# First stage of a graph network with two columns of nodes per transposition and per matmul

## The chip, the cores and the metric

The kernel runs on one NeuronCore of a Trainium2 chip. Times are device microseconds (us). Three runs of the kernel before took 4300.02, 4304.88 and 4320.17 us; the median is 4304.88 us. The engines are named PE (TensorE, matmuls), ACT (ScalarE), DVE (VectorE), POOL (GpSimd) and SP (SyncE, which here only issues DMAs). Each engine works through its own instructions in the order in which they were laid down; engines wait for one another through semaphores.

## What is computed

One layer of a message-passing graph network with attention, on 12,500 nodes of 64 features and 412,500 edges sorted by receiver:

```
h  = relu(layernorm(x))
m  = concat(h[src], h[dst], edge)                 # 64 + 64 + 32 features
messages = silu(m @ W1 + b1) @ W2 + b2            # 64
logit    = silu(m @ Wa1 + ba1) @ Wa2 + ba2        # 1
att      = softmax(logit over all edges)
agg      = segment_sum(messages * att, dst)
out = x + silu(concat(h, agg) @ Wu1 + bu1) @ Wu2 + bu2
```

The products of m with W1 and Wa1 split into a part of the sender, a part of the receiver and a part of the edge. So the kernel makes two tables of 128 values per node first: ts = h @ [Wa1, W1] of the sender's rows, and tr of the receiver's rows, and then adds, for each edge, one row of ts, one of tr and the edge's own product.

## The kernel before

**Stage one, the tables.** The nodes are padded to 12,544 and laid out as 128 partitions of NB = 98 columns: column b of all partitions is a set of 128 nodes. They are worked in 7 chunks of CB = 14 columns. The loop at L200 normalises a chunk: DVE sums it (L205) and subtracts the mean (L208), ACT squares (L210), DVE sums again (L212), ACT takes the root (L214), DVE inverts (L215) and multiplies with the relu in one pass, giving h (L217). Then, in blocks of four columns, PE transposes each column of h (L224), DVE copies the four transposed columns from PSUM to the tile hT (L225), PE multiplies each with the sender's weights (L228), and ACT copies the result from PSUM to the tile ts (L230). hT has 65 rows: 64 features and a row of ones (L184, a memset on POOL), through which the matmul adds the biases, which are the last row of w_node (L98 to L109). At the end of a chunk SP stores ts to the table ts_d in DRAM (L231), and ACT's queue stores hT to hT_d (L232), to be read again much later by `node_bias`.

A second loop (L233) multiplies the same hT, column by column, with the receiver's weights (L240), DVE copies the results (L242), and ACT's queue stores them to tr_d (L243). `keep_in_program_order` holds these matmuls behind those of the first loop.

`windows()` (L186 to L198) computes from the receivers' numbers where each edge's receiver lies in its window: eight DVE instructions, the largest over 128 x 3224 values (L188). It is called ahead of the third chunk.

**Stage two, the edges.** `one_pass` takes 403 groups of K = 8 x 128 edges. For each group POOL issues eight indirect DMAs (L358), each of which gathers 128 rows of ts_d by the senders' numbers into the tile gs, of which there are 8 buffers. Edges are sorted by receiver, so a group's receivers lie in a window of tr_d that SP loads (L377); DVE builds a one-hot matrix (L379) and one matmul per 256 edges (L385) gives the receiver's and the edge's parts together. DVE adds them to gs (L390), ACT takes the tanh (L391), DVE forms the messages and logits (L399 to L407), and some groups later a weighted sum into the nodes follows (L442 to L481). Every fourth group from the 16th on also runs `node_bias` (h @ Wu1 + bu1 for four columns of nodes, from hT_d) or `node_rest`. A last stage updates the nodes (L572 on).

**What sets the order.** The program is written as above, but a planner lays down each engine's list by its own estimate of when things are ready, within the dependences, except where `keep_in_program_order` (`pin`) fixes it. So DVE, ACT and SP have the instructions of neighbouring chunks mixed, and where a call stands in the text is not where its instructions stand in the list. DMAs of SP and of ACT go to two queues, which share the 16 DMA engines, and each DMA instruction takes one of eight semaphores in turn, so that an issue can also wait for an earlier DMA of the same semaphore. The gathers wait for the whole of ts_d, since any edge can ask for any row.

Of the kernel before, what the change touches and what calls it, by code (L numbers as in the profile page):

```python
# [40 lines left out]
F32 = mybir.dt.float32  # L42
I32 = mybir.dt.int32
AF = mybir.ActivationFunctionType
ALU = mybir.AluOpType
# [5 lines left out]
P = 128  # L51
D = 64
DE = 32
U = 64
C = 2 * U
# [19 lines left out]
def gnn_kernel(ctx: ExitStack, tc: tile.TileContext, n_edges, x, src, dst, dst_row, first, edge,  # L75
# [14 lines left out]
    hT_d = dram.tile([D, NB, P], F32, name="hT_d")  # L90
# [7 lines left out]
    w_node = const.tile([D + 1, 2 * C + U], F32, name="w_node")  # L98
    nc.vector.memset(w_node[D:D + 1, C:2 * C], 0.0)
    nc.sync.dma_start(w_node[:D, 0:U], Wa1[0:D, :])  # L100
    nc.sync.dma_start(w_node[:D, U:C], W1[0:D, :])
    nc.sync.dma_start(w_node[D:D + 1, 0:U], ba1[None, :])
    nc.sync.dma_start(w_node[D:D + 1, U:C], b1[None, :])
    nc.scalar.dma_start(w_node[:D, C:C + U], Wa1[D:2 * D, :])
    nc.scalar.dma_start(w_node[:D, C + U:2 * C], W1[D:2 * D, :])
    nc.scalar.dma_start(w_node[:D, 2 * C:], Wu1[0:D, :])
    nc.scalar.dma_start(w_node[D:D + 1, 2 * C:], bu1[None, :])

    nc.vector.tensor_scalar(w_node[:, 0:2 * C], w_node[:, 0:2 * C], 0.5, None, op0=ALU.mult)  # L109
# [12 lines left out]
    def across(ap, n, name, dtype=F32, parts=P):  # L122
        t = const.tile([parts, n], dtype, name=name)
        nc.scalar.dma_start(t, bass.AP(tensor=ap.tensor, offset=ap.offset, ap=[[0, parts], [1, n]]))
        return t

    wa2 = across(Wa2, U, "wa2")
# [40 lines left out]
    with tc.tile_pool(name="node1", bufs=1) as node1, \  # L168
# [14 lines left out]
        hT = node1.tile([D + 1, NB, P], F32, name="hT")  # L183
        nc.gpsimd.memset(hT[D:D + 1], 1.0)  # L184
# [14 lines left out]

        for c in range(0, NB, CB):  # L200
            if c == min(2 * CB, NB - CB):
                windows()
# [17 lines left out]
            for b in range(0, CB, 4):  # L220
                n = min(4, CB - b)
                pt = node_ps.tile([D, 4, P], F32, name="pt")
                for i in range(n):
                    nc.tensor.transpose(pt[:, i, :], h[:, b + i, :], ident)  # L224
                nc.vector.tensor_copy(hT[:D, c + b:c + b + n, :], pt[:, :n, :])  # L225
                pn = node_ps.tile([P, 4, C], F32, name="pn")
                for i in range(n):
                    nc.tensor.matmul(pn[:, i, :], hT[:, c + b + i, :], w_node[:, 0:C],  # L228
                                     start=True, stop=True)
                nc.scalar.copy(ts[:, b:b + n, :], pn[:, :n, :])  # L230
            nc.sync.dma_start(ts_d.rearrange("(p b) f -> p b f", b=NB)[:, c:c + CB, :], ts)  # L231
            nc.scalar.dma_start(hT_d[:, c:c + CB, :], hT[:D, c:c + CB, :])  # L232
        for c in range(0, NB, CB):  # L233
            tr = node.tile([P, CB, C], F32, name="tr")
            for b in range(0, CB, 4):
                n = min(4, CB - b)
                pn = node_ps.tile([P, 4, C], F32, name="pn")
                for i in range(n):
                    tc.keep_in_program_order(
                        nc.tensor.matmul(pn[:, i, :], hT[:, c + b + i, :], w_node[:, C:2 * C],  # L240
                                         start=True, stop=True))
                nc.vector.tensor_copy(tr[:, b:b + n, :], pn[:, :n, :])  # L242
            nc.scalar.dma_start(tr_d[:NP, :].rearrange("(p b) f -> p b f", b=NB)[:, c:c + CB, :], tr)  # L243
# [8 lines left out]
def node_bias(tc, b, v, work, ps):  # L252

    nc = tc.nc
    NB, w_node = v["NB"], v["w_node"]
# [3 lines left out]
    nc.sync.dma_start(hb[:D, :n, :], v["hT_d"][:, b:b + n, :])  # L259
    pb = ps.tile([P, 4, P], F32, name="mt")  # L260
    nc.tensor.matmul(pb[:U, :n, :], w_node[:, 2 * C:], hb[:, :n, :], start=True, stop=True)
# [570 lines left out]
```

## Time and profile before

| | |
|---|---|
| median of three runs | 4304.88 us |
| the profiled execution | 4310.41 us |
| its span, first to last instruction | 4308.7 us |
| POOL busy | 3166.1 us (73%), 3237 instructions |
| DVE busy | 2544.5 us (59%) |
| PE busy | 2221.4 us (52%) |
| ACT busy | 595.8 us (14%) |
| first gather starts | 85.41 us |
| last copy into ts ends | 78.93 us |

A busy PE is not a PE at its peak, since matmuls overlap. Waits are idle time of an engine ahead of an instruction, put down to the event that released it; "issue" is time in which nothing that the profile shows was waited for. A group of instructions is read as: line, engine, operation, output<-inputs, count, busy time and mean, idle time before them. An f32 matmul leaves two records on PE, so 98 matmuls of a pass are 196 records; a transposition leaves one.

### The profile page before, as it was taken

To read this page: it belongs to the slowest core of one execution; us is meant where nothing else is said; L and a number is where in the kernel's file an instruction comes from. 1 tells how busy PE (TensorE), PEld (TensorE's weight loads), DVE (VectorE), ACT (ScalarE), POOL (GpSimd) and SP (SyncE) were. 2 spreads that over 40 slices of the span, in tenths; PEclk is the share of its full clock that TensorE was granted. 3 is DMA by queue.
4 is the path that set the end of the run, shared out by engine and by line. 5 is a ranking of instruction groups with operands and counts; after the bars stand their busy time and mean duration, and the time that the engine had idled before them with its cause. 6 is when DMAs were issued, how large, how long until landed. Compare 5 with 4: busy or idle time off the path is not lost.

```text
span 4308.7 us, 41469 instructions
## 1 busy us (share of the span) xinstructions
PE 2221.4 (52%) x11224; PEld 1681.3 (39%) x11224; DVE 2544.5 (59%) x4914; ACT 595.8 (14%) x1212; POOL 3166.1 (73%) x3237
## 2 busy tenths in 40 slices
PE   6644544644445555544444555555554444545554
PEld 6533333433334434433333334444343333334443
DVE  6755655655556555556555565555565555655557
ACT  2211111111111111111111111111111111111113
POOL 2777777777777777777777777777777777777771
PEclk8657676576766555666666665555566666665555
DMA  6533334333333333333333333333333333333323
GB/s 199 144 81 96 94 96 99 92 97 93 97 93 80 86 87 78 88 88 78 87 84 81 88 80 85 87 78 88 88 78 87 84 81 88 80 86 87 78 75 101
DMA packets 227005, 391.95 MB, mean 91 GB/s; under 512 B 98890, under 2 KB 151179, under 8 KB 213707
## 3 DMA queue, kind: packets, MB, share of 16 engines
q0 software_dynamic: 103168, 211.49, 20.1%
q1 hardware_dynamic: 120580, 167.79, 15.0%
q10 hardware_dynamic: 3014, 9.92, 0.8%
q8 instruction: 93, 1.52, 0.2%
q14 instruction: 150, 1.22, 0.1%
HBM read 363.16 MB, written 25.72 MB: 90 GB/s over the span
## 4 chain that ended last, share of the span: by engine, by line
POOL 42%; issue 26%; DMA 14%; DVE 9%; PE 8%; DVEq 0%; ACT 0%; ACTq 0%; POOLq 0%; SPq 0%
POOL gs L358 42%; DMA gs<-ts_d,src_sb 13%; PE pe L385 5%; DVE eo L379 2%; PE sp L456 2%; DVE gs L390 1%; DVE att L404 1%; DVE sums L481 1%; PE mt L467 1%; DVE sums L480 1%; PE pn L228 1%; DVE uT L586 1%; DVE lg L407 0%; DVE wt L452 0%; DVE oh L442 0%
## 5 line engine op out<-in xcount | busy, mean ns | idle before, releaser
L358 POOL DMA_INDIRECT gs<-ts_d,src_sb x3224 | 3154.0, 978 | 1054.6 <-issue 900.8
L385 PE MATMUL pe<-wins,eo 128*128 128x256 f32 x3224 | 1348.6, 591 | 1248.7 <-issue 1170.2
L385 PEld LDWEIGHTS pe<-wins,eo 128*128 128x128 f32 x3224 | 926.1, 301 | 1514.2 <-issue 1216.5
L390 DVE TENSOR_TENSOR gs<-pe,gs 128x1024 f32<-128x1024 f32 x403 | 491.5, 1220 | 1398.2 <-DMA gs<-ts_d,src_sb 1394.5
L391 ACT ACTIVATE pe<-gs 128x1024 f32<-128x1024 f32 x403 | 413.4, 1026 | 2962.2 <-DVE gs L390 2661.2
L456 PE MATMUL sp<-wt,acts 128*65 128x40 f32 x6448 | 581.7, 260 | 3.0 <-DVE wt L452 3.0
L456 PEld LDWEIGHTS sp<-wt,acts 128*65 128x65 f32 x6448 | 531.1, 172 | 28.3 <-DVE wt L452 3.5
L422 PE MATMUL mt<-ident,mx 128*128 128x128 f32 x102 | 48.4, 474 | 676.2 <-DVE sums L480 668.1
L399 DVE SCALAR_TENSOR_TENSOR acts<-pe,gs 128x512 f32<-128x512 f32 x403 | 275.4, 683 | 56.7 <-ACT pe L391 56.7
L422 PEld LDWEIGHTS mt<-ident,mx 128*128 128x128 f32 x102 | 18.5, 182 | 688.8 <-DVE sums L480 679.9
L404 DVE TENSOR_TENSOR att<-att,wa 128x512 f32<-128x512 f32 x403 | 277.6, 689 | 9.7
L407 DVE TENSOR_REDUCE lg<-att 128x8 f32<-128x512 f32 x403 | 275.0, 682 | 10.3
L379 DVE TENSOR_TENSOR eo<-db,bj 64x512 f32<-64x512 int32 x403 | 275.9, 685 | 7.3
L402 DVE SCALAR_TENSOR_TENSOR att<-pe,gs 128x512 f32<-128x512 f32 x403 | 273.4, 678 | 0.0
L467 PEld LDWEIGHTS mt<-ss,w2u 65*64 65x64 f32 x806 | 97.5, 171 | 292.0 <-issue 223.2
L452 DVE TENSOR_TENSOR wt<-oh,p 128x320 f32<-128x320 f32 x403 | 197.3, 490 | 9.8
L442 DVE TENSOR_TENSOR oh<-dloc,iota_w 128x320 f32<-128x320 f32 x403 | 192.1, 477 | 0.1
L467 PE MATMUL mt<-ss,w2u 65*64 65x40 f32 x806 | 147.8, 276 | 68.2 <-ACT ss L462 42.3
L477 DVE SCALAR_TENSOR_TENSOR sums<-sums,scale,mt 64x40 f32 x102 | 25.3, 248 | 167.5 <-PE mt L467 167.5
L481 DVE COPY sums<-nmax 64x40 f32 x403 | 77.2, 192 | 9.3 <-issue 0.2
L433 ACT ACTIVATE scale<-fall 128x1 f32<-128x1 f32 x102 | 20.7, 203 | 427.0 <-DVE fall L432 427.0
L462 ACT COPY ss<-sp 65x40 f32<-65x40 f32 x403 | 73.5, 182 | 23.8 <-PE sp L456 23.2
(97 smaller groups left out, 763.6 us busy)
## 6 DMA issues: line engine op xcount, KB each, us to landing
gs<-ts_d,src_sb POOLq DMA_INDIRECT x3224
eo<-in_edge_dram SPq DMA_DIRECT2D x100, 512.0 KB
db<-in_dst_row_dram SPq DMA_DIRECT2D x200, 256.0 KB
wins<-tr_d SPq DMA_DIRECT2D x806, 32.0 KB
ts_d<-ts SPq DMA_DIRECT2D x7, 896.0 KB
tr_d<-tr ACTq DMA_DIRECT2D x7, 896.0 KB
xc<-in_x_dram SPq DMA_DIRECT2D x7, 448.0 KB
hT_d<-hT ACTq DMA_DIRECT2D x7, 448.0 KB
```

The lines of the kernel that those rows point to most:

```text
L358: nc.gpsimd.indirect_dma_start(out=gs[:, j, :], out_offset=None, in_=ts_d[:, :], in_offset=bass.IndirectOffsetOnAxis(ap=src_sb[:, t + j:t ...
L379: pin(nc.vector.tensor_tensor(eo[:WR, :].rearrange("p (h e) -> p h e", h=2), db.rearrange("p (h e) -> p h e", h=2), bj[:, g, :, None].to_b ...
L385: pin(nc.tensor.matmul(pe[:, 2 * q:2 * q + 2, :], eo[:, q * P:(q + 1) * P], win[:, q // 2, :, :], start=True, stop=True))
L390: pin(nc.vector.tensor_tensor(gss[g], pes[g], gss[g], ALU.add))
L391: pin(nc.scalar.activation(pes[g], gss[g], AF.Tanh))
L399: pin(nc.vector.scalar_tensor_tensor(acts[g % ACTS][:, :, 0:U], th[:, :, U:C], 1.0, gs[:, :, U:C], op0=ALU.add, op1=ALU.mult))
L402: pin(nc.vector.scalar_tensor_tensor(att, th[:, :, 0:U], 1.0, gs[:, :, 0:U], op0=ALU.add, op1=ALU.mult))
L404: pin(nc.vector.tensor_tensor(att, att, wa2[:, None, :].to_broadcast([P, K, U]), ALU.mult))
L407: pin(nc.vector.tensor_reduce(lgs[s][:, k:k + K], att, AX.X, ALU.add))
L452: pin(nc.vector.tensor_tensor(wt, ohs.pop(g), ps_[batch[g]][:, k:k + K, None].to_broadcast([P, K, W]), ALU.mult))
L456: pin(nc.tensor.matmul(sp, acts[g % ACTS][:, j, :], wt[:, j, :], start=j == 0, stop=j == K - 1))
L467: pin(nc.tensor.matmul(pp, w2u, sps.pop(g), start=True, stop=True))
```

## The change

- Two neighbouring columns of h, 128 x 128 values, go into one transposition. hT becomes 128 rows (features of the even column above those of the odd one) by 49 pairs.
- One matmul takes such a pair: its weights w_pair are 128 x 2 x 128, the sender's weights in the upper rows for the first column and again in the lower rows for the second, zeros elsewhere, so it yields 256 values per node pair. The same for the receiver's weights.
- The row of ones, POOL's memset of it and the bias row go. The biases, halved like the weights, are loaded across all partitions and are added where the receiver table's results leave PSUM: the copy becomes an addition.
- The copy of the transposed columns moves from DVE to ACT; blocks are now of four pairs. The tile pn has three buffers instead of two.
- hT_d is stored once, after the loop, and `node_bias` reads each half of it with a DMA of its own; its weights are a tile of their own, w_bu.
- `windows()` is called after the first loop.

In the order laid down, the first load of x now stands ahead of the weights on SP's queue. ACT's list has 23 DMA issues ahead of its first square where it had 19. DVE's list has the copy of the transposed w2b (L342 in the new numbering) ahead of the first variance reduction; before it stood behind the receiver pass. The subtraction over 128 x 3224 stands ahead of the third h. The single store of hT_d stands on ACT's list ahead of the last four copies into ts.

```diff
-    hT_d = dram.tile([D, NB, P], F32, name="hT_d")
+    hT_d = dram.tile([2 * D, NB // 2, P], F32, name="hT_d")
...
-    w_node = const.tile([D + 1, 2 * C + U], F32, name="w_node")
...
+    w_pair = const.tile([P, 2, 2, C], F32, name="w_pair")
+    nc.vector.memset(w_pair, 0.0)
+    for r in range(2):
+        for h, eng in ((0, nc.sync), (1, nc.scalar)):
+            rows = slice(h * D, (h + 1) * D)
+            eng.dma_start(w_pair[rows, r, h, 0:U], Wa1[r * D:(r + 1) * D, :])
+            eng.dma_start(w_pair[rows, r, h, U:C], W1[r * D:(r + 1) * D, :])
+    w_bu = const.tile([D + 1, U], F32, name="w_bu")
+    nc.scalar.dma_start(w_bu[:D, :], Wu1[0:D, :])
+    nc.scalar.dma_start(w_bu[D:D + 1, :], bu1[None, :])
...
+    bias = const.tile([P, C], F32, name="bias")
+    for ap, c in ((ba1, 0), (b1, U)):
+        nc.scalar.dma_start(bias[:, c:c + U],
+                            bass.AP(tensor=ap.tensor, offset=ap.offset, ap=[[0, P], [1, U]]))
...
-        hT = node1.tile([D + 1, NB, P], F32, name="hT")
-        nc.gpsimd.memset(hT[D:D + 1], 1.0)
+        hT = node1.tile([2 * D, NB // 2, P], F32, name="hT")
...
+        nc.vector.tensor_scalar(w_pair, w_pair, 0.5, None, op0=ALU.mult)
         for c in range(0, NB, CB):
-            if c == min(2 * CB, NB - CB):
-                windows()
...
-            for b in range(0, CB, 4):
-                n = min(4, CB - b)
-                pt = node_ps.tile([D, 4, P], F32, name="pt")
-                for i in range(n):
-                    nc.tensor.transpose(pt[:, i, :], h[:, b + i, :], ident)
-                nc.vector.tensor_copy(hT[:D, c + b:c + b + n, :], pt[:, :n, :])
-                pn = node_ps.tile([P, 4, C], F32, name="pn")
-                for i in range(n):
-                    nc.tensor.matmul(pn[:, i, :], hT[:, c + b + i, :], w_node[:, 0:C],
-                                     start=True, stop=True)
-                nc.scalar.copy(ts[:, b:b + n, :], pn[:, :n, :])
+            for b in range(0, CB, 8):
+                n = min(8, CB - b)
+                q = (c + b) // 2
+                pt = node_ps.tile([P, 4, P], F32, name="pt")
+                for i in range(n // 2):
+                    nc.tensor.transpose(pt[:, i, :], h[:, b + 2 * i:b + 2 * i + 2, :], ident)
+                nc.scalar.copy(hT[:, q:q + n // 2, :], pt[:, :n // 2, :])
+                for i in range(0, n, 4):
+                    m = min(4, n - i)
+                    pn = node_ps.tile([P, 4, C], F32, name="pn", bufs=3)
+                    for k in range(0, m, 2):
+                        nc.tensor.matmul(pn[:, k:k + 2, :], hT[:, q + (i + k) // 2, :], w_pair[:, 0],
+                                         start=True, stop=True)
+                    nc.scalar.copy(ts[:, b + i:b + i + m, :], pn[:, :m, :])
             nc.sync.dma_start(ts_d.rearrange("(p b) f -> p b f", b=NB)[:, c:c + CB, :], ts)
-            nc.scalar.dma_start(hT_d[:, c:c + CB, :], hT[:D, c:c + CB, :])
+        nc.scalar.dma_start(hT_d, hT)
+        nc.vector.tensor_scalar(bias, bias, 0.5, None, op0=ALU.mult)
+        windows()
         for c in range(0, NB, CB):
...
-                pn = node_ps.tile([P, 4, C], F32, name="pn")
-                for i in range(n):
+                pn = node_ps.tile([P, 4, C], F32, name="pn", bufs=3)
+                for i in range(0, n, 2):
                     tc.keep_in_program_order(
-                        nc.tensor.matmul(pn[:, i, :], hT[:, c + b + i, :], w_node[:, C:2 * C],
+                        nc.tensor.matmul(pn[:, i:i + 2, :], hT[:, (c + b + i) // 2, :], w_pair[:, 1],
                                          start=True, stop=True))
-                nc.vector.tensor_copy(tr[:, b:b + n, :], pn[:, :n, :])
+                nc.vector.tensor_tensor(tr[:, b:b + n, :], pn[:, :n, :],
+                                        bias[:, None, :].to_broadcast([P, n, C]), ALU.add)
...
-    nc.sync.dma_start(hb[:D, :n, :], v["hT_d"][:, b:b + n, :])
+    for r in range(2):
+        nc.sync.dma_start(hb[:D, r:n:2, :], v["hT_d"][r * D:(r + 1) * D, b // 2:(b + n) // 2, :])
```

## The prediction

> **What bounds the kernel now.** I read the waits of GpSimd (POOL) first, then the groups, the timeline of the first 90 us, and the durations of single records. Waits of POOL (us in total, times, longest):
>
> ```profile
> POOL gs L358 <- issue: 900.8, 2956, 0.3
> POOL gs L358 <- DMA ts_d<-ts: 72.4, 1, 72.4
> POOL gs L358 <- DVE eo L379: 42.7, 140, 0.3
> ```
>
> After one wait of 72.4 us for the sender table ts_d, no gather waits longer than 0.3 us, which is the gap between any two gathers: POOL never stands. The group of gathers says what that costs (count | busy us, mean ns | idle before):
>
> ```profile
> L358 POOL DMA_INDIRECT gs<-ts_d,src_sb x3224 | 3154.0, 978 | 1054.6 <-issue 900.8
> ```
>
> So the span is a sum of three: first gather at 85.41; 3224 gathers, 3154.0 busy plus 3223 gaps of some 0.305 (982.2), to 4221.6; a tail of 87.1 to 4308.7. The change touches only what lies ahead of the first gather, and its price is how far that moves. The timeline of that part (start, length, engine, what):
>
> ```profile
> 2.46 10.54 POOL L184 MEMSET hT<- 1x12544 f32 x1
> 4.00 9.15 DVE L109 TENSOR_SCALAR w_node<-w_node 65x256 f32<-65x256 f32 x1 [2.52 <-DMA w_node<-in_b_dram]
> ...
> 15.95 0.95 ACT L210 ACTIVATE sq<-xm 128x896 f32<-128x896 f32 x1
> ...
> 20.23 0.29 PE L331 MATMUL mt<-ident,w2b 65*64 65x65 f32 x1 [20.23 <-DMA w2b<-in_W_dram]
> ...
> 22.47 1.09 DVE L217 SCALAR_TENSOR_TENSOR h<-xm,rstd 128x896 f32<-128x896 f32 x1
> ...
> 78.96 0.32 SPq L231 DMA_DIRECT2D ts_d<-ts  x1
> ...
> 85.41 1.10 POOL L358 DMA_INDIRECT gs<-ts_d,src_sb  x1 [72.40 <-DMA ts_d<-ts]
> ```
>
> The reader should see: a vector instruction that ends with POOL's memset; ScalarE's first square at 15.95, behind 19 DMA issues on its queue; the weight w2b landing only at 20.2; seven chunks from 22.5 to 78.9; and 6.4 us from the last copy into ts to the first gather.
>
> **What PE pays for.** Durations of single matmul records, min/median/max ns, in three stretches:
>
> ```profile
> L228 PE MATMUL pn<-w_node,hT x5: 421/421/553, 26.4 to 27.4; 65*128 65x128 f32 x5
> L228 PE MATMUL pn<-w_node,hT x10: 274/275/422, 49.6 to 51.0; 65*128 65x128 f32 x10
> L240 PE MATMUL pn<-w_node,hT x15: 421/421/582, 89.6 to 92.9; 65*128 65x128 f32 x15
> ```
>
> PE is slow (421) until about 50, fast (275) from 50.4 to 81, and slow again, although the clock column of a table by stretches gives 1.00 before 50 too. Starts of successive records lie 0.213 us apart slow and 0.108 fast for 128 moving columns; for the 256-column matmuls of L385 it is 0.427 and 0.216. An f32 matmul has two such records, a transposition one; weight loads are hidden, also those of 128 columns.
>
> **The change, part by part.**
> *Pairing matmuls*: 98 x 2 x 0.213 becomes 49 x 2 x 0.427, both 41.8 us slow: nothing, in the sender pass and in the receiver pass alike. What is saved is instructions, not columns.
> *Pairing transpositions*: 98 to 49 records, 10.5 us slow, 5.3 fast. PE per chunk falls from 14 x 0.213 + 28 x 0.213 = 8.96 to 7 x 0.213 + 14 x 0.427 = 7.47 slow, 4.5 to 3.8 fast.
> *Copies to ScalarE*: VectorE loses 21 x 0.68 + 7 x 0.41 = 17.1 us and keeps per chunk two reductions, two subtract/multiply passes and small ones, 4.9 us. ScalarE gains 7 x (0.59 for 512 columns + about 0.48 for 384, between its 0.59 and 0.37 rows) = 7.5 us, 4.4 per chunk.
> *Bias to the receiver table*: 28 evictions become additions with one PSUM operand; L390, the same kind at 1024 columns, takes 1220 ns, so 512 stays at the copies' 0.69. Nothing; they lie after the table that the gathers wait for. If the receiver pass (PE 41.8 slow, evictions 17.4) is no faster than its 43.9 now, it still begins and ends earlier than now. The buffers of 8 groups need it 64 x 1.25 = 80 us after the first gather, and now group 0 is released at 147.2 against 165.4: 18 us of cover that grows, as the pass starts some 12 us earlier, by no less than the gathers do.
> *POOL's memset gone, x loaded first*: VectorE's first mean can start at about 4 instead of 13.1. But behind it stand ScalarE's DMA issues, 23 instead of 19 (0.7 us each): first square about 19 instead of 15.95. And in VectorE's program order the copy of the transposed w2b (in the trace at 136.6) now stands ahead of the first variance reduction, so everything behind it, first h included, waits for w2b, whose load sits four issues further back (two of them 128-row broadcasts). It lands at 20.2 now; four issues at 0.6 make it 22.5 (20 to 25). First h: 22.8 + two reductions 2.1, four short steps and hand-overs 1.2, h 1.1 = 27.2, against 23.6 now. The early start is more than given back.
> *Receivers' places later*: written after the loop, but the planned VectorE order has the 3.52 us subtraction ahead of the third h, the rest (2.9) between later ones: the 6.4 us stay ahead of the last h. Nothing.
> *hT_d as one store* of 3.2 MB (128 rows of 25,088 bytes) on ScalarE's queue, issued ahead of the last four ts copies, in place of seven of 0.46 MB. A 7,168-byte packet takes 0.27, so 8 packets per engine of 0.95 = 7.6 us. Priced below.
> *node_bias*: 25 more small loads, 0.5 us each on SP, which waits 1972.9 us for PE in its window loads: hidden; uncovered 13 us of SP time spread over 1000.
>
> **The sum up to the last copy.** I walked VectorE's, ScalarE's and PE's lists in program order with these durations, 0.08 us per hand-over. The same walk over the old lists, PE fast from 50.4, ends at 78.7; the trace has 78.93. For the new lists (w2b at 22.5, fast from 35) the chunks' h end at 27.2, 29.4, 39.6, 46.3, 48.5, 54.0, 58.7 and their last ts copies at 36.5, 41.0, 45.4, 51.5, 57.1, 61.7, 66.1. Between 29.4 and 39.6 lie the 3.5 us subtraction and four chunk-wide passes; later squares stand on ScalarE behind copies that wait for PE, so a slow PE now holds back VectorE too.
>
> **When PE gets fast** decides most. Rows: busy without a gap from 84.7 to 122 with 65 rows, it stayed slow; the full 128 x 128 weights of L385 from 138.4 made it fast at 142.5, within 4 us. The new first chunk is 6 us of full-size matmuls. [...] I take L385's row, 35.
>
> **From the last copy to the first gather.** Alone, a ts store starts 0.83 us after its issue, moves for 2.4, and the gather follows 1.24 after: 4.5. In the trace four of seven started some 2 us after issue, when the hT_d store issued just before was at its last packets. By that row the last ts store starts with the eighth hT_d packet: hT_d issued 62.8, moving 63.9, eighth at 70.6, ts 2.9 more, 1.24: first gather 74.7. If the two stores took turns packet by packet (0.95 and 0.27), ts would end at 73.6, the same within 0.2. Unobstructed the first gather would be at 70.6. I take 74.9.
>
> First gather 85.4 to 74.9: -10.5. The profiled run took 4310.4 (4308.7 span plus 1.7); the median of the runs is 4304.9, 5.5 lower, and I apply the shift to that: 4294.4.
>
> **Rivals.**
> *PE stays slow* through the stage. For: 37 us of L240. Against: L385. Last copy 84.5, hT_d then issued 78.3, first gather 90.1: +4.7, 4310, slower than before. It decides from PE becoming fast after about 65.
> *No obstruction and w2b early* (20.2, hT_d not ahead): 67.8, -17.6, 4287. For: the first ts store, alone, started in 0.83. Against: four of seven.
> *The gathers' own pace*: beyond 0.943 each they lose 115.6 us in all to neighbours, and the groups from 300 to 1500 us, where node_bias runs, lose about twice the rest. A fifth more or less is 23 us either way, 4271 or 4317. The work beside them is nearly the same, so little for it.
> *Nothing comes of it*: a late w2b (25) and PE fast at 65: 86.4, 4306.
>
> **Chances.** Likeliest 0.62 (its own range 4288 to 4301: w2b 20 to 25, PE fast 30 to 50); PE slow or nothing 0.15; full gain 0.11; pace 0.12, halved by sign. With some 4 us for the median's own spread, 8 in 10 lie within 4283 and 4312. 0.5% is 21.5 us, about what a measurement of this kernel can tell from no change; the stage could give it only with a first gather before 63.9. Faster by more: 0.10, from the pace and the edge of full gain; slower by more: 0.06, from the pace; within: 0.84.
>
> **What would show it.** First gather at 71 to 79, its 0.3 us gaps and 87 us tail unchanged; w2b's copy on VectorE near 22 with idle time before it; 256-column records 0.427 apart, then 0.216 from 30 to 42; the last ts store starting some 3 us late behind hT_d. Wrong if any gather after the first waits over a microsecond, if the mean gather leaves 970 to 985 ns, or if the first gather is outside 68 to 91.

## Result and profile after

| | before | after | difference |
|---|---|---|---|
| median of five runs, us | 4304.88 (4300.02 to 4320.17) | 4290.06 (4282.16 to 4292.41) | -14.8 |
| profiled execution: time, us | 4310.41 | 4292.41 | -18.0 |
| its span, us | 4308.7 | 4290.7 | -18.0 |
| first gather at | 85.41 | 74.74 | -10.67 |
| 3224 gathers, busy | 3154.04 | 3145.69 | -8.35 |
| 3223 gaps between them | 982.17 | 982.31 | +0.1 |
| tail after the last gather | 87.06 | 87.95 | +0.9 |

The ratio of the runs is 0.9946, with a 95% interval from 0.9929 to 0.9963: between 16 and 31 us faster, 23 in the middle; this is not the quotient of the medians, which differ by 14.8 us, and the means differ by 20.7. The forecast of 4294.4 lies 4 us from the median and its first gather, 74.9, is met within 0.2 us; but its gain of 10.5 us is under half of what the ratio says and lies outside its interval. The table says where the profile sees more: in the busy time of the gathers, which the forecast had put at no change.

The costliest group of the page after, the gathers (count | busy us, mean ns | idle before), and the waits of POOL (us in total, times, longest):

```profile
L367 POOL DMA_INDIRECT gs<-ts_d,src_sb x3224 | 3145.7, 976 | 1054.6 <-issue 886.6 <-DMA tr_d<-tr 72.3 <-DMA gs<-ts_d,src_sb 63.1
```

```profile
POOL gs L367 <- issue: 886.6, 2909, 0.3
POOL gs L367 <- DMA tr_d<-tr: 72.3, 1, 72.3
POOL gs L367 <- DMA gs<-ts_d,src_sb: 63.1, 207, 0.3
POOL gs L367 <- DVE eo L388: 16.8, 55, 0.3
```

POOL still never stands: after the first wait no gap is longer than 0.3 us. So the sum of three (start, gathers, tail) holds for this profile as for the one before. The mean gather went from 978 to 976 ns, which looks like nothing and is 8 us over 3224 of them.

The timeline of the first stage after (start, length, engine, what):

```profile
4.17 1.09 DVE L207 TENSOR_REDUCE mean<-xc 128x14 f32<-128x896 f32 x1 [2.40 <-DMA xc<-in_x_dram]
...
20.38 0.29 PE L340 MATMUL mt<-ident,w2b 65*64 65x65 f32 x1 [20.38 <-DMA w2b<-in_W_dram]
20.70 0.22 DVE L342 COPY w2t<-mt 64x65 f32<-64x65 f32 x1 [3.64 <-PE mt L340]
21.57 1.79 ACT L212 ACTIVATE sq<-xm 128x896 f32<-128x896 f32 x2
22.55 2.08 DVE L214 TENSOR_REDUCE rstd<-sq 128x14 f32<-128x896 f32 x2 [1.62 <-ACT sq L212]
...
25.27 1.09 DVE L219 SCALAR_TENSOR_TENSOR h<-xm,rstd 128x896 f32<-128x896 f32 x1
...
60.38 0.35 ACTq L237 DMA_DIRECT2D hT_d<-hT  x1
...
63.80 0.32 SPq L236 DMA_DIRECT2D ts_d<-ts  x1
...
74.74 1.10 POOL L367 DMA_INDIRECT gs<-ts_d,src_sb  x1 [72.34 <-DMA tr_d<-tr]
```

Before, the first mean waited until POOL's memset was over; now it starts at 4.17. That buys nothing, as forecast: the first variance reduction starts at 22.55 (forecast: h behind two reductions that begin at 22.8), and the first h ends at 26.36 against 23.56 before. The last store into ts_d is issued at 63.80 and the gather follows only 10.9 us later. (The row names tr_d as the last thing waited for. The gathers read ts_d alone; the store of ts_d has its last packets at 73.0 in the trace.)

PE's matmul records by stretches (instructions: min/median/max ns, first and last start):

```profile
L233 PE MATMUL pn<-w_pair,hT x10: 633/634/796, 29.1 to 33.1; 128*128 128x256 f32 x10
L233 PE MATMUL pn<-w_pair,hT x83: 378/379/581, 33.5 to 61.8; 128*128 128x256 f32 x83
L247 PE MATMUL pn<-w_pair,hT x40: 378/379/380, 63.1 to 71.6; 128*128 128x256 f32 x40
L247 PE MATMUL pn<-w_pair,hT x13: 634/635/796, 75.7 to 80.9; 128*128 128x256 f32 x13
L247 PE MATMUL pn<-w_pair,hT x45: 378/379/527, 81.4 to 92.5; 128*128 128x256 f32 x45
```

The first ten 256-column records take 634 ns, the later ones of the sender pass 379. The receiver pass, which was slow before, is fast too, but for 13 records behind a pause of PE from 72 to 75.7. PE got fast at 33.5, within the first chunk, a little ahead of the forecast's 35.

### The profile page after: what moved, and what is told of

Same layout as the page of the kernel before. It is cut to its first block, busy times and chain, and to the rows that moved or that the text cites. A ratio compares the mean times of both kernels' runs of the same rounds, so it can differ in the third digit from the quotient of the medians.

```text
span 4290.7 us, 40985 instructions
## 1 busy us (share of the span) xinstructions
PE 2150.5 (50%) x10979; PEld 1624.4 (38%) x10979; DVE 2521.7 (59%) x4887; ACT 601.8 (14%) x1226; POOL 3147.2 (73%) x3236
## 3 DMA queue, kind: packets, MB, share of 16 engines
q1 hardware_dynamic: 125808, 167.82, 14.8%
## 4 chain that ended last, share of the span: by engine, by line
POOL 44%; issue 24%; DMA 15%; PE 8%; DVE 7%; DVEq 0%; ACT 0%; POOLq 0%; ACTq 0%
POOL gs L367 44%; DMA gs<-ts_d,src_sb 14%; PE pe L394 5%; PE sp L465 2%; DVE eo L388 1%; DVE gs L399 1%; DVE att L413 1%; PE mt L476 1%; DVE lg L416 1%; DVE uT L595 1%; DVE sums L490 0%; DVE wt L461 0%; DVE sums L489 0%; DVE oh L451 0%; DVE att L411 0%
## 5 line engine op out<-in xcount | busy, mean ns | idle before, releaser
L367 POOL DMA_INDIRECT gs<-ts_d,src_sb x3224 | 3145.7, 976 | 1054.6 <-issue 886.6
L394 PE MATMUL pe<-wins,eo 128*128 128x256 f32 x3224 | 1318.9, 581 | 1265.0 <-issue 1171.9
L394 PEld LDWEIGHTS pe<-wins,eo 128*128 128x128 f32 x3224 | 911.8, 297 | 1521.8 <-issue 1233.2
L442 ACT ACTIVATE scale<-fall 128x1 f32<-128x1 f32 x102 | 20.7, 203 | 426.5 <-DVE fall L441 426.5
## 6 DMA issues: line engine op xcount, KB each, us to landing
hT_d<-hT ACTq DMA_DIRECT2D x1, 3136.0 KB
```

The costliest lines, as they stand in the source:

```text
L367: nc.gpsimd.indirect_dma_start(out=gs[:, j, :], out_offset=None, in_=ts_d[:, :], in_offset=bass.IndirectOffsetOnAxis(ap=src_sb[:, t + j:t ...
L394: pin(nc.tensor.matmul(pe[:, 2 * q:2 * q + 2, :], eo[:, q * P:(q + 1) * P], win[:, q // 2, :, :], start=True, stop=True))
```

## The experiments

The runs were made in five sittings, each on one chip, and these were of two kinds. In the fifth, as in the two profiles above, POOL never stands and the kernel before takes 4303 us. In the other four it takes 5373 to 5485 us, because there POOL does stand: 123 to 138 times in each profile, 1030 to 1170 us in all. A run is therefore compared only with the runs of the kernel before in its own sitting, and what a run tells depends on the kind. The chip of the second sitting and of the fifth has the same number, so it is not said that the kind belongs to the chip.

### Is the busy time of the gathers scatter, and is it node_bias

The two kernels again, unchanged, and the kernel before with one part of the change: the two loads of hb in place of one.

> The changed kernel once more, nothing edited. In its first trace the gathers start at 74.7 us (85.4 before) and then take 3145.7 us of POOL time in all (3154.0 before), so of the span's 18.0 us the start gives 10.7 and the gathers' pace 8.4, with 0.9 lost in the tail. Theory 1, the pace is scatter from execution to execution and the change gives only the start: a second trace starts at 73 to 76 again, its busy time of the gathers lies anywhere from 3140 to 3160, and over many runs the mean difference from the kernel before comes down to 9 to 13 us. Theory 2, the change also makes the gathers faster: the busy time is 3146 within 3 again, and the difference stays at 18 to 23 us.

> The kernel before once more, nothing edited. Theory 1 (scatter): gathers start at 84 to 87, their busy time is anywhere from 3140 to 3160, and the runs lie within 4298 to 4320 as the five of before do. Theory 2 (the change makes the gathers faster): busy time 3154 within 3 again, clearly above that of both traces of the changed kernel.

```
-    nc.sync.dma_start(hb[:D, :n, :], v["hT_d"][:, b:b + n, :])
+    for r in range(2):
+        nc.sync.dma_start(hb[:D, r:n:2, :], v["hT_d"][:, b + r:b + n:2, :])
```

> The kernel before with one part of the change alone: node_bias loads its four columns of hT_d in two DMAs, even and odd columns, instead of one. The first stage is untouched, so the gathers start at 84 to 87. If the two loads are what alters the gathers' pace (theory 2a), the time falls by 8 to 12 us and the gathers' busy time goes to 3146. If they are hidden behind SP's waits for PE, as I forecast, the time is that of the kernel before within 0.2% and the busy time is not told from its scatter.

| | time, us | ratio, 95% | first gather | gathers busy | gaps |
|---|---|---|---|---|---|
| before_again | 5373.53 | 1.0000 [0.9972, 1.0027] | 84.18 | 3133.2 | 2034.5 |
| after_again | 5338.38 | 0.9937 [0.9914, 0.9960] | 74.53 | 3130.6 | 2008.9 |
| before_hb2 | 5382.43 | 1.0027 [0.9997, 1.0057] | 88.68 | 3134.2 | 2044.9 |

The two loads bring no gain here. (The first gather of before_hb2 came 4.5 us later than in before_again, outside what was expected, with the same lists in the first stage; what delayed it was not found.) The busy times lie together, but the test is weaker than it was meant to be, for scatter and for the two loads alike: in this sitting POOL is not the bound, its gaps are twice as long, and the change gains 35 us where the start moved by 10. What the other 25 us are in such a sitting had to be found first.

### What the change gains where POOL stands

Two kernels took the start apart from the rest: the changed kernel with its start held back to that of the kernel before, and the changed kernel with its start moved further ahead by the order of two stores.

```
             nc.vector.scalar_tensor_tensor(h, xm, 0.0, ...)
+            if c == NB - CB:
+                for _ in range(20):
+                    nc.vector.tensor_scalar(h, h, 1.0, None, op0=ALU.mult)
```

> The changed kernel with 20 multiplications by 1.0 in place on the last chunk's h, each about 0.58 us by the 993 ns of 1612 columns: they only hold back the start, by 11 to 12 us, so the first gather is at 85 to 87. If the time is first gather plus a fixed pace plus tail, the time rises by the same 11 to 12 us (0.25%). If the gathers' pace depends on where the first of them falls against the other engines' work, their busy sum moves by more than 5 us with it. If something other than GpSimd sets the end, the time rises by less than half of the delay.

```
-            nc.sync.dma_start(ts_d..., ts)
-        nc.scalar.dma_start(hT_d, hT)
+            tc.keep_in_program_order(
+                nc.sync.dma_start(ts_d..., ts))
+        tc.keep_in_program_order(nc.sync.dma_start(hT_d, hT))
```

> The changed kernel with the one store of hT_d put on SP's queue behind the last store of ts, instead of on ScalarE's queue ahead of the last four copies into ts. If that store delays the last ts store as I priced it (first gather 74.9 with it, 70.6 without), the ts store now starts about 0.8 us after its issue and the first gather comes 3.5 to 4.5 us earlier, at 70 to 71.5, and the time falls by as much. If the two stores share the DMA engines without delay, the first gather stays at 74 to 75.

| | ratio, 95% | first gather | POOL stands at gathers 64 to 88 | gather 96 starts |
|---|---|---|---|---|
| before_again | 1.0000 [0.9972, 1.0027] | 84.2 | 48.4 | 253.3 |
| after_again | 0.9937 [0.9914, 0.9960] | 74.5 | 15.1 | 210.1 |
| after_hT_late | 0.9956 [0.9936, 0.9975] | 69.1 | 28.5 | 218.7 |
| after_hold (second sitting) | 0.9936 [0.9915, 0.9957] | 84.1 | 15.6 | 220.7 |

With its start held back to 84.1 the changed kernel is still 35 us faster than the one before, so where POOL stands most of the gain is not the start. It is not nothing either: in the three sittings that have both, the held kernel is 10 to 20 us slower than the changed one, by the medians and by the ratios, for a start 9.8 us later. And moving the start 5.4 us ahead by the order of the stores (expected: 3.5 to 4.5) gained no time, since the stand at the 64th gather grew by 13. The forecast had this place, "the buffers of 8 groups need it 64 x 1.25 = 80 us after the first gather", with a cover of 18 us. Here the cover is gone. The timeline of POOL in the kernel before, and of VectorE in the receiver pass shortly before it:

```profile
94.07 0.69 DVE L242 COPY tr<-pn 128x512 f32<-128x512 f32 x1 [1.58 <-PE pn L240]
97.64 0.69 DVE L242 COPY tr<-pn 128x512 f32<-128x512 f32 x1 [2.88 <-remote]
100.45 0.42 DVE L242 COPY tr<-pn 128x256 f32<-128x256 f32 x1 [2.13 <-PE pn L240]
110.26 0.69 DVE L242 COPY tr<-pn 128x512 f32<-128x512 f32 x1 [9.38 <-remote]
128.45 0.69 DVE L242 COPY tr<-pn 128x512 f32<-128x512 f32 x1 [17.50 <-remote]
```

```profile
161.72 0.94 POOL L358 DMA_INDIRECT gs<-ts_d,src_sb  x1 [0.30 <-issue]
162.96 0.94 POOL L358 DMA_INDIRECT gs<-ts_d,src_sb  x1 [0.30 <-issue]
212.64 0.94 POOL L358 DMA_INDIRECT gs<-ts_d,src_sb  x1 [48.73 <-issue]
```

The copies of the receiver pass come every 1.7 us in the profile before (0.69 and 1.01 of waiting); here they come 3, then 10, then 18 us apart and up to 22, some of them 38 us behind the last record of their block. POOL stands still from 163.9 on; from 174.6 they come every 1.7 again. So the receiver table is complete at 191 instead of 123, and the 64th gather waits for it by way of its buffer. If gathers under way make the hand-over from PE to VectorE late, holding back the gathers alone should help:

```
-            nc.sync.dma_start(ts_d..., ts)
+            for _ in range(7 if c == NB - CB else 1):
+                nc.sync.dma_start(ts_d..., ts)
```

> The kernel before with the store of the last chunk of ts_d repeated six more times, each after the one before it: nothing but the first gather is held back, by 6 x 3.5 to 4.5 = 21 to 27 us, to 106 to 112, while the receiver pass goes on. Theory, the late hand-overs from PE to VectorE of 8 to 22 us that the runs of GpSimd standing at the 64th gather show come only with gathers under way: the receiver pass then goes through at its 1.7 us per copy and ends by 125 to 130, the stand at the 64th gather (47 to 49 us so far) falls under 15 us, that gather starts at 188 to 200 instead of 212, and the kernel gets faster by 10 to 25 us though it starts 21 to 27 us later. Rival, the late hand-overs have nothing to do with the gathers: the stand stays and the kernel gets slower by up to 27 us. Where GpSimd never stands: slower by the 21 to 27 us.

```profile
112.09 0.42 DVE L243 COPY tr<-pn 128x256 f32<-128x256 f32 x1 [0.16 <-PE pn L241]
114.10 0.69 DVE L243 COPY tr<-pn 128x512 f32<-128x512 f32 x1 [1.58 <-PE pn L241]
115.81 0.69 DVE L243 COPY tr<-pn 128x512 f32<-128x512 f32 x1 [1.01 <-PE pn L241]
116.49 1.10 POOL L359 DMA_INDIRECT gs<-ts_d,src_sb  x1 [103.48 <-DMA ts_d<-ts]
```

The first gather came 31.5 us later than in before_again3 beside it (116.5 against 85.0; each repeated store took 5 us, not 3.5 to 4.5). The receiver pass ran through at its 1.7 us per copy and ended at 125, the stand at the 64th gather was gone, gather 96 started at 241.9 against 253.8, and the time was 0.9986 [0.9970, 1.0003] of the kernel before: a start 31 us later cost nothing. The expectation named 10 to 25 us of gain and got 3, part of it given back because the start moved by more than planned and because gather 96 gained only 12. The mechanism stands, in this one pair: in such a sitting the copies are late only where gathers have been running for some microseconds (9 in before_again). Why, and why not in the fifth sitting, no run here shows.

The change has eight of the 28 copies of the receiver pass done before the first gather, where the kernel before has four, and its copies waited for at most 11 us in after_again. That is where the 30 to 40 us come from here: gather 96 starts 43 us earlier in after_again than in before_again, 33 of it from the stand. All profiles in which POOL stands agree: with 21 copies done before the first gather there is no stand up to gather 88 (before_gate), with eight it is 12 to 21 us, with five 28 to 41, with three or four 46 to 48. Repeats in sittings of this kind:

> The changed kernel once more, for the scatter between profiles. If the 8 us by which its gathers' busy time was smaller are scatter, the first gather is again at 74 to 76 while the busy sum of the 3224 gathers falls anywhere in some 3130 to 3160 us; if the change itself makes the gathers shorter, the sum is within 3 us of 3145.7 where GpSimd never stands.

> The kernel before once more. Where GpSimd never stands (no gap above 0.6 us): first gather 84 to 86, and if the busy sum of the gathers is a matter of scatter it falls at 3130 to 3160 us, not at 3154 again. Where GpSimd does stand: its first stand, at the 64th gather, of 40 to 50 us, because vector instructions of the receiver pass start only 8 to 22 us after the matmul before them.

> The changed kernel once more. Where GpSimd never stands: first gather 74 to 75; by the start alone the time is 10.5 us below the kernel before, by the measured ratio some 21. Where it does stand: a stand of 2 to 16 us at the 64th gather, and 35 to 50 us below the kernel before.

> The changed kernel held back by 20 vector instructions, again. Where GpSimd never stands: first gather near 84.1, as the kernel before; if all of the gain is the start, the time is within 3 us of the kernel before; if the change has a second source that does not lie ahead of the first gather, the time is 8 to 12 us below it. Where GpSimd stands: 30 to 40 us below, as in the first such run.

> The kernel before, for the profile beside the others. Where GpSimd never stands: first gather 84 to 86, busy sum of the gathers within 3130 to 3160 if it is scatter, at 3151 to 3157 if it belongs to the kernel. Where it stands: 46 to 49 us at the 64th gather.

> The changed kernel, likewise. Where GpSimd never stands: busy sum within 3130 to 3160 if it is scatter, at 3143 to 3149 if it belongs to the kernel, and a time 10.5 us below the kernel before by the start alone. Where it stands: first stand 2 to 16 us, 35 to 50 us below.

> The changed kernel held back by 20 vector instructions, first gather near 84.4. Where GpSimd never stands: within 3 us of the kernel before if all of the gain is the start, 8 to 12 us below it if the change has a second source behind the first gather. Where it stands: 29 to 36 us below, as twice before.

| sitting | run | ratio, 95% | first gather | stands to gather 88 | gathers busy |
|---|---|---|---|---|---|
| second | after_again2 | 0.9913 [0.9892, 0.9934] | 74.4 | 13.4 | 3124.6 |
| third | before_again2 | 0.9988 [0.9968, 1.0008] | 85.7 | 46.5 | 3139.5 |
| third | after_again3 | 0.9914 [0.9890, 0.9939] | 74.8 | 14.4 | 3138.0 |
| third | after_hold2 | 0.9946 [0.9925, 0.9967] | 84.6 | 20.9 | 3132.0 |
| fourth | before_again3 | 1.0001 [0.9985, 1.0018] | 85.0 | 47.1 | 3147.4 |
| fourth | after_again4 | 0.9923 [0.9898, 0.9948] | 74.9 | 20.1 | 3136.0 |
| fourth | after_hold3 | 0.9960 [0.9943, 0.9977] | 84.7 | 20.4 | 3147.5 |

after_hold3 fell short of what was expected (21 us below by the ratio, not 29 to 36), and after_hold2 just (29, not 30 to 40). The kernel before has its busy time at 3133.2 in one profile and at 3147.4 in another of the same chip: where POOL stands, that sum scatters by 14 us and does not tell the kernels apart.

### When PE gets fast

The kernel before with hT and w_node filled up to 128 rows, the additional rows ones times zero weights, so that the sums are the same:

```
-    w_node = const.tile([D + 1, 2 * C + U], F32, name="w_node")
-    nc.vector.memset(w_node[D:D + 1, C:2 * C], 0.0)
+    w_node = const.tile([P, 2 * C + U], F32, name="w_node")
+    nc.vector.memset(w_node[D:, :], 0.0)
...
-        hT = node1.tile([D + 1, NB, P], F32, name="hT")
-        nc.gpsimd.memset(hT[D:D + 1], 1.0)
+        hT = node1.tile([P, NB, P], F32, name="hT")
+        nc.gpsimd.memset(hT[D:], 1.0)
```

> The kernel before, with hT and w_node filled up from 65 to 128 rows (ones times zero weights), nothing else. Theory A, matmuls over all 128 rows make PE fast and those over 65 rows do not: records of the sender pass fall from 421 to about 275 ns some 8 us after the first of them, at about 34 instead of 50, the receiver pass becomes fast too (its 98 matmuls take some 22 us of PE instead of 42, VectorE's 0.69 us copies then set its length), and the first gather comes 3 to 5 us earlier than the kernel before has it. Theory B, something else (the time since the start, the weights' form) makes PE fast: 421 ns until about 50 again, first gather at 84 to 86.

```profile
L228 PE MATMUL pn<-w_node,hT x28: 421/421/551, 26.2 to 37.4; 128*128 128x128 f32 x28
L228 PE MATMUL pn<-w_node,hT x168: 275/275/348, 39.5 to 74.7; 128*128 128x128 f32 x168
L240 PE MATMUL pn<-w_node,hT x108: 275/275/377, 75.2 to 92.2; 128*128 128x128 f32 x108
L240 PE MATMUL pn<-w_node,hT x50: 421/421/582, 96.3 to 175.1; 128*128 128x128 f32 x50
L240 PE MATMUL pn<-w_node,hT x38: 274/275/421, 175.3 to 180.4; 128*128 128x128 f32 x38
```

The same instructions in number and columns, over 128 rows instead of 65, are fast from 39 instead of 50 on, and in the receiver pass too, where 65 rows are slow, as long as the blocks follow one another. From 96 on, where blocks of this sitting come up to 22 us apart, they are slow, and fast again at 175.5, 4.2 us after the blocks closed up at 171.3. That is theory A, though five microseconds later than it said: the first chunk, 5 us of work from 26.2 to 31.0, was not enough, and it came 4.2 us into the second, which began at 34.9. The first gather came at 81.97, some 3 us ahead of the kernel before in other sittings, and the ratio is 0.9967 [0.9952, 0.9982] where POOL stands. The stand at the 64th gather was still 41 us: eight records of a block are 1.7 us of PE even when slow, of up to 22 us between copies, so it is the hand-overs, not the matmuls, that make the receiver pass late there.

### What sets the first h

Nine of ScalarE's issues go to GpSimd's queue: three in `across` (Wa2, ba2, bu2), two for bias, two for w2b, and wu1a and wu2.

```
-        nc.scalar.dma_start(t, bass.AP(...))
+        nc.gpsimd.dma_start(t, bass.AP(...))
...
-    nc.scalar.dma_start(w2b[:U, :], W2)
-    nc.scalar.dma_start(w2b[U:S1, :], b2[None, :])
+    nc.gpsimd.dma_start(w2b[:U, :], W2)
+    nc.gpsimd.dma_start(w2b[U:S1, :], b2[None, :])
...
-    nc.scalar.dma_start(wu2, Wu2)
+    nc.gpsimd.dma_start(wu2, Wu2)
```

> Nine of ScalarE's 23 DMA issues (bias, Wa2, ba2, bu2, w2b, wu1a, wu2) go to GpSimd's queue. Theory A, ScalarE's own issue list sets the first square and with it the first h: first square at 9 to 11 instead of 21.6, first h ends at 18 to 21 instead of 26.4, and since only the first two chunks gain all of it, the last copy into ts comes 2 to 6 us earlier and the first gather at 69 to 73 instead of 74.6. Theory B, as forecast, the load of w2b sets it: the planner's list now has the copy of w2b behind the first h, so B too gives an early h; but then the first square stays near 20. Either way less than 7 us: 0.05 to 0.15% of the time.

The first square started at 11.92 instead of 21.57, the first h ended at 19.3 instead of 26.4, the last store of ts_d was issued 7.8 us earlier (56.04) and the first gather came at 66.92, a little better than expected. The copy of w2b came at 25.8 and held up nothing. In this kernel the copy of w2b also no longer stands ahead of the first variance reduction, so the run alone cannot part the two; the timeline of after does: w2b's copy was over at 20.92 and the reduction still waited 1.62 us for the square. So ScalarE's own list of 23 issues was late, and not the landing of w2b. The ratio was 0.9884 [0.9859, 0.9908], against 0.9913 for the changed kernel beside it: 7 us in the median, as the start says.

### Both, and the sitting in which POOL never stands

Loads on GpSimd's queue and hT_d's store last, together:

> The changed kernel with the nine loads on GpSimd's queue and the store of hT_d behind the last store of ts_d. Both gains in the start are on different stretches, so they add up: first gather at 61 to 64 (74.5, less 7.5 by the loads, less 5.4 by the store). Where GpSimd never stands the time falls by the same 11 to 13 us below the changed kernel; where it stands at the 64th gather, the store's part comes back as a longer stand there and only the 7 us of the loads are left.

In the third sitting: first gather 62.04 as expected, 5342.72 us against 5349.00 for after_again3, a stand of 30.6 us at the 64th gather. In the last sitting POOL never stands, and there the second source can be seen again:

> The changed kernel with nine loads on GpSimd's queue and hT_d's store last, again. First gather at 62. Where GpSimd never stands: 12 to 13 us below the changed kernel beside it. Where it stands: a stand of some 30 us at the 64th gather, so that 0 to 8 us are left.

> The changed kernel beside it. First gather 74 to 75. Where GpSimd never stands: 10.5 us below the kernel before if the start is all, and a busy sum of the gathers that need not be 3146 again (3125 to 3160). Where it stands: 26 to 52 us below the kernel before.

| | median, us | ratio, 95% | first gather | gathers busy | beyond 0.943 each | gathers over 1.0 us |
|---|---|---|---|---|---|---|
| profile before | | | 85.41 | 3154.0 | 115.6 | 439 |
| profile after | | | 74.74 | 3145.7 | 107.4 | 426 |
| kernel before, beside the two below | 4302.77 (15 runs) | | | | | |
| after_again5 | 4289.16 (10 runs) | 0.9966 [0.9951, 0.9980] | 75.17 | 3144.2 | 105.9 | 421 |
| after_best2 | 4259.73 (6 runs) | 0.9893 [0.9875, 0.9911] | 62.68 | 3127.0 | 88.7 | 303 |

The changed kernel's busy sum came back within 1.5 us. Of the kernel before there is only the one profile of this kind, and its execution, 4310.41, lies 5 us above the mean of its 20 runs here. And after_best2, whose start is 12.5 us earlier, is not 12 to 13 us faster, as expected, but 29.4 (spans 4289.8 and 4259.8: 12.5 from the start, 17.2 from the gathers, 0.3 from gaps and tail). From about the 420th DVE instruction on, all engines have the same list in both kernels. So the same edge loop runs at another pace when what lies ahead of it differs. The group of gathers in both:

```profile
L367 POOL DMA_INDIRECT gs<-ts_d,src_sb x3224 | 3144.2, 975 | 1055.0 <-issue 889.9 <-DMA tr_d<-tr 72.8 <-DMA gs<-ts_d,src_sb 61.9
```

```profile
L368 POOL DMA_INDIRECT gs<-ts_d,src_sb x3224 | 3127.0, 970 | 1037.2 <-issue 888.2 <-DMA ts_d<-ts 54.8 <-DMA gs<-ts_d,src_sb 42.4
```

Where a gather loses its time shows when each is set beside what VectorE does meanwhile. First after_again5, then after_best2, in the same stretch of the timeline:

```profile
3054.64 0.48 DVE L451 TENSOR_TENSOR oh<-dloc,iota_w 128x320 f32<-128x320 f32 x1
3054.87 1.06 POOL L367 DMA_INDIRECT gs<-ts_d,src_sb  x1 [0.30 <-DVE eo L388]
3055.17 0.48 DVE L461 TENSOR_TENSOR wt<-oh,p 128x320 f32<-128x320 f32 x1
3056.24 0.94 POOL L367 DMA_INDIRECT gs<-ts_d,src_sb  x1 [0.31 <-issue]
```

```profile
3060.18 0.48 DVE L452 TENSOR_TENSOR oh<-dloc,iota_w 128x320 f32<-128x320 f32 x1
3060.58 0.94 POOL L368 DMA_INDIRECT gs<-ts_d,src_sb  x1 [0.30 <-issue]
3060.69 0.49 DVE L462 TENSOR_TENSOR wt<-oh,p 128x320 f32<-128x320 f32 x1
3061.83 0.94 POOL L368 DMA_INDIRECT gs<-ts_d,src_sb  x1 [0.30 <-issue]
```

The multiplication wt starts 0.30 us after its gather in one and 0.11 in the other; the first gather takes 1.06, the second 0.94. Sorted over the 400 wt of each trace that begin before the last gather, by how long after the start of a gather they begin, the mean length of that gather is:

| wt begins after the gather's start by | before: count, mean us | after | after_again5 | after_best2 |
|---|---|---|---|---|
| 0.00 to 0.15 | 15, 0.945 | 13, 0.944 | 21, 0.943 | 89, 0.944 |
| 0.15 to 0.30 | 45, 1.044 | 134, 1.022 | 137, 1.024 | 83, 0.970 |
| 0.30 to 0.45 | 124, 1.130 | 58, 1.144 | 46, 1.146 | 25, 1.159 |
| 0.45 to 0.60 | 25, 1.031 | 16, 1.079 | 18, 1.065 | 19, 1.057 |
| 0.60 to 0.75 | 48, 0.944 | 33, 0.943 | 34, 0.944 | 48, 0.955 |
| 0.75 to 0.90 | 37, 1.220 | 51, 1.227 | 53, 1.228 | 43, 1.231 |
| 0.90 to 1.05 | 52, 1.311 | 47, 1.291 | 46, 1.263 | 53, 1.254 |
| later | 54, 1.150 | 48, 1.079 | 45, 1.096 | 40, 1.022 |
| lost beyond 0.943, first three rows | 27.7 us | 22.2 | 20.5 | 7.8 |
| lost beyond 0.943, all these gathers | 70.7 us | 61.8 | 59.4 | 42.6 |
| lost beyond 0.943, the other 2824 | 44.9 us | 45.5 | 46.5 | 46.1 |

The last two rows place the difference: gathers in which no wt begins lose the same in all four traces, and the whole change lies in the 400. Most of it is in the first three rows. There the price rises steadily from 0.15 us on, and cut into steps of 0.05 us the four traces agree on it within 0.03 (0.95 to 0.98 us at 0.15 to 0.20, 1.24 to 1.25 at 0.45 to 0.50, and 0.94 to 0.95 again from 0.50 on); what differs is how many fall where. The bulk moves from the third row to the second to the first. In the rows from 0.60 on, the comparison oh, which comes shortly ahead of wt, begins in most of the same gathers, so that their price is not wt's alone. What makes wt costly is open: the multiplication att<-att,wa, which reads two tiles of SBUF as wt does, begins 0.15 to 0.50 us into 347 gathers of the four traces, and none of these takes more than 0.947.

VectorE's place is tied to the gathers, because in the later part of the trace it waits for them (from 3000 to 3600 us of after, VectorE's addition of gs waits 45 times and 220 us for a group's last gather to land). From the end of that gather to the addition it is 1.68 us before, 1.61 after (both profiles) and 1.52 in after_best2, tenth percentile from 1500 us on, and the bulk of wt moves by as much. What changes that landing was not found; after_best2 also has nine loads on the queue of the gathers, so its earlier start is not the only candidate. No run moved wt alone: the tie of place and price is read from the traces.

## Why the prediction was right or wrong

*What bounds the kernel: right.* In the two profiles of the result the gaps are the same to 0.1 us and POOL stands nowhere; the span is start plus gathers plus tail.

*First gather 85.4 to 74.9: right, 74.74, with two errors that cancel, which is luck.* The walk gave the last ts copy at 66.1; it ended at 63.8, as each chunk's h came 1 to 2 us earlier than walked. From that copy to the first gather the forecast had 8.6 us and it took 10.9. The last ts store, issued at 63.80, had its first packets at 68.0, when the sixth of hT_d's eight per engine ended, and its last at 73.0: it did not start with the eighth packet and then run free in 2.9, but took turns with the last two of hT_d (0.93 us a packet, against 0.27 of its own) and then with the first store of tr_d. The direction (obstructed by hT_d) is shown by after_hT_late, where the store alone had the gather 4.6 us after its issue (forecast for that: 4.5) and the first gather came at 69.1.

*w2b sets the first h: wrong in the cause, near in the time.* The first h ended at 26.36, forecast 27.2, and the reduction ahead of it did start at 22.55, but behind ScalarE's squares. Its issue list lasted until 20.3, a table load took 1.28 us more, and the first square started at 21.57 instead of the forecast "about 19". w2b's copy was over at 20.9.

*Pairing matmuls saves nothing in itself, PE fast from 35, copies to ScalarE: right.* PE got fast at 33.5, 4.4 us after the first full matmul (29.1) and a little ahead of the forecast's 35, which it had by L385's row (4.1 us, 138.4 to 142.5). That PE could be fast from 30 on, as the forecast's range and its signs had it, rests on no trace; the profile after shows 33.5. In the thirteen profiles of the changed kernel and its variants the first faster record comes 1.4 us (after_poolq, 22.61 from 21.16) to 5.7 us (after_hold3, 34.97 from 29.26) after the first full matmul, so L385's 4 us lies among them, but no single time fits them all. Matmuls over 65 rows in the receiver pass do not follow L385's row: they stayed at 421 ns through 37 us without a gap, and before_k128 made the same columns fast (275 ns) by filling the rows alone. In the sender pass 65 rows were fast (275 ns) from 50 to 81; there transpositions stand between them, and what part these have in it was not tried apart. The bias additions took 0.69 us for 512 columns, as forecast.

*node_bias hidden: not contradicted.* before_hb2 shows no gain and, at 0.9997 to 1.0057, at most a small loss, but where POOL stands; it was not run where the gathers set the end. after_again5 and after_best2 both have the two loads and differ by 17 us in the gathers.

*The gathers' own pace: the step that failed.* The forecast priced it ("beyond 0.943 each they lose 115.6 us", "a fifth more or less is 23 us") and put it at nothing, because "the work beside them is nearly the same". The work is; when it falls within a gather is not. The loss went from 115.6 to 107.4 us in the profile after and 105.9 in the repeat: 7 to 8% of it, 8 to 10 us. With the 10.7 of the start, less 1.0 for gaps and tail, that is the 18 us of the spans. The forecast's own sign for it, a mean gather outside 970 to 985 ns, was 48 us wide over 3224 gathers and could not show it.

The runs give a smaller size, as the profile before was of an execution above the mean. Over both comparisons in which POOL never stands, the kernel before has a mean of 4305.5 us (20 runs, spread over 27 us with nothing changed) and the changed one 4289.3 (15 runs): 16.2 us apart, 12 to 20 by their spreads. Less some 10.5 for the start and with 1.0 for the tail, an estimate of 7 us is left for the pace, 3 to 11. So the second source is there in the runs too, its place (wt within the gather) is read from the traces, and why it shifted is open. The forecast's 10.5 lies inside the interval of the repeat (9 to 21 us) and outside that of the first comparison.

*Rivals.* PE slow: refuted by the records. No obstruction and an early w2b, with 4287 at 67.8: not what happened; after_best2, with both removed, has its first gather at 62.7. The gathers' pace, with 0.12: it was part of the outcome, at about a third of the fifth named.

## What to carry to other kernels

When one engine runs back to back to the end, as POOL does where it never stands, a start moved ahead counts in full (10.7 us in the profile after, 12.5 in after_best2), but the pace is a term too: in these traces its cost sits in who is working beside each instruction (a gather takes 0.944 to 1.25 us by where wt begins in its first 0.5 us), and a shift of a consumer by a tenth of a microsecond against a periodic producer (1.61 to 1.52 us) goes with 17.2 us, more than the 10.5 that the edit itself was priced at. Look at the engine's mean duration to the nanosecond and multiply by the count before calling it unchanged. And cover that is read from one profile, such as 18 us at the 64th gather, should be seen in a second sitting before it is priced at nothing.

## What the runs showed of the hardware

- f32 matmuls of 128 columns over 65 rows stayed at 421 ns per record through 37 us without a gap (84.7 to 121.8, profile before). The same over 128 rows took 275 from 39.5 on in before_k128, 421 again from 96 to 175, where blocks came up to 22 us apart, and 275 once they had followed closely for 4.2 us. A median over a long stretch hides such steps; they are found by cutting the stretch finer.
- In four of five sittings VectorE's copies of PE's results in the receiver pass came 3 to 22 us apart instead of 1.7, from 5 to 11 us after indirect gathers had begun to be issued back to back, and every 1.7 again 11 us after these stopped (before_again); in the fifth never. The kernel before takes 5373 to 5485 us there instead of 4303.
- In the profiles before and after, after_again5 and after_best2, a gather of 0.944 us takes up to 1.25 when the VectorE multiplication wt (0.49 us) begins 0.15 to 0.50 us after its start, more the later it begins, and 0.944 when it begins within 0.15. Another multiplication of two SBUF tiles, att<-att,wa, does nothing of the kind (347 gathers, none above 0.947).
- A last store of 0.9 MB issued 3.4 us after one of 3.2 MB on another queue had its first packet 4.2 us after its issue and its last after 9.2 (profile after); ahead of it (after_hT_late), the gather followed its issue by 4.6.
